# Gates r and z of a GRU as seven block products instead of eight, in a graph-network kernel on one core

## The chip, the core and the metric

The kernel runs on one core of a Trainium2 chip. The metric is the device time of one execution in microseconds (us). A core has five engines that run side by side, each in its own order: TensorE (PE in the profile: matmuls; PEld: its weight loads), VectorE (DVE), ScalarE (ACT), GpSimd (POOL) and SyncE (SP, which here only starts transfers). Matmuls write to PSUM, in banks of 128 partitions x 512 float32; all else lies in SBUF.

## The reference, cut to what matters

64 graphs with 256 nodes and 256 features, float32 throughout. Layer 0 multiplies each graph by its normalised adjacency matrix and a weight, adds the input and normalises (layernorm). Layer 1 makes three things of the result x: a convolution over the nodes with 17 taps (x_conv), messages weighted by a distance (x_nmp), and a GRU cell, which the change is about:

```
x_in = concatenate([x_conv, x_nmp])          # 256 nodes x 512
gi = x_in @ w_ih.T + b_ih                    # 256 x 768: parts r, z, n
gh = x @ w_hh.T + b_hh                       # 256 x 768
r = sigmoid(gi_r + gh_r)
z = sigmoid(gi_z + gh_z)
n = tanh(gi_n + r * gh_n)
out = layernorm(x + (1 - z) * n + z * x)
```

For r and z the hidden and the input part are only added. So both gates together are one product: inputs (256 nodes x 768: x, x_nmp, x_conv) times weights (768 x 512).

## The kernel before, in words

The 64 graphs go in four quarters of Q = 16. `layer0` (L314) and `layer1` (L379) do everything of a graph up to the messages, and write three things to DRAM: x1 (`x1_d`), the gates' inputs x and x_nmp transposed (`xn_d`), and, in SBUF, the Fourier transform, in blocks of nodes, of the convolution's first step (`V`, L436). When a quarter is through, the convolution is done for all its graphs at once: `products` (L504) multiplies each of the 24 frequencies by its weights, streamed from DRAM (`load_u`, L476, on SP's queue); `real_transform` and `complex_begin` start the inverse transform, and `complex_end` (L669) does its rest on VectorE, in 18 pieces, with 16 outputs that go to DRAM (`output`, L655, `xc_d`). Then come the quarter's gates, `gru` (L730), one graph after another: 4 pieces per graph.

`gru` before: for each chunk c of 128 nodes, six matmuls of 128 x 128 weights by 128 x 512 give r and z together in one PSUM bank (L748), and six of half that width give the two parts of n in another (L759). VectorE adds the bias (L763), ScalarE takes tanh (L764; a sigmoid by tanh of half the argument), GpSimd makes z + 3 and multiplies x1 by it (L766, L767), VectorE joins the parts of n (L769 to L773), ScalarE takes its tanh (L776), and VectorE and ScalarE finish with the layernorm (L787 to L789). The convolution reaches the gates by `load_conv` (SP), `residual` (a DMA that adds x1, issued by GpSimd, L715) and `transposed` (four transposes, L726, and two relus on ScalarE, L728, into `xcT`).

What orders the work: each stage is a generator that yields between pieces, and `merge`, `take` and `both` weave them by hand. `AHEAD` graphs (8 before) of the next quarter run layer 0 and 1 during the current quarter's convolution, with their transform in a second buffer `V2`, which is copied into V (L925) when the inverse has left it. The other graphs of the next quarter then run beside the first 4 gates (`early`), and the other 12 gates (`late`) run beside the next quarter's products and inverse. The last quarter has no next one: its gates run alone, at the end. The framework places the waits, gives out buffers, and draws up each engine's order from priorities in the order of the code, so work that is ready can be pulled ahead of its place: the first L748 matmuls run at 413.5 us, while the first inverse outputs (L664) are at 427.3.

PSUM is split into four banks for graphs (`bank`) and four for products and gates (`accbank`).

Of the kernel before, what the change touches and what calls it, by code (L numbers as in the profile page):

```python
# [9 lines left out]
F32 = mybir.dt.float32  # L10
# [4 lines left out]
P = 128  # L15
# [11 lines left out]
def kernel(  # L27
# [47 lines left out]
    loads = ctx.enter_context(tc.tile_pool(name="loads", bufs=3))  # L75
# [42 lines left out]
    unused = const.tile([P, N], F32)  # L118
# [5 lines left out]
    scols = []  # L124
    for i in range(2):
        t = const.tile([P, NCH, P], F32, name=f"scols{i}")
        nc.gpsimd.memset(t, 0.0)
        for c in (NSE, 32 + NSE):
            nc.gpsimd.memset(t[:, :, c : c + 1], 1.0)
        scols.append(t)  # L130

    wih = const.tile([P, 2 * DCH, 3 * D], F32)
    whh = const.tile([P, DCH, 3 * D], F32)
    brz_t = const.tile([P, 2 * D], F32)
# [179 lines left out]
    def layer0(g):  # L314

        a_t, x_t = ain.pop(g), xin.pop(g)


        deg = small.tile([P, NCH], F32, name="deg")
        if g < 2:  # L320
            nc.vector.tensor_reduce(deg, a_t, AX.X, ALU.add)
        else:
            for c in range(NCH):
                nc.scalar.activation(unused, a_t[:, c, :], AF.Copy, accum_out=deg[:, c : c + 1])
# [8 lines left out]
        adjT = work.tile([P, NCH, 3, P], F32, name="adjT", bufs=3)  # L333
        ADJT[g] = adjT
# [44 lines left out]
    def layer1(g, V, place):  # L379
# [23 lines left out]
        cols = scols[g % 2].rearrange("p c (q r) -> p c q r", r=32)  # L403
# [39 lines left out]
        for c in range(NCH):  # L443
            nc.tensor.transpose(p[:, c * P : (c + 1) * P], scols[g % 2][:, c, :], ident)
# [132 lines left out]
    def turned(re, im, angle):  # L577


        t = freq.tile([P, 2, D], F32, name="turn", bufs=4)  # L580
        x, y = M[:, re, :], M[:, im, :]
        real_part(t[:, int(re > im), :], x, y, angle)
        return imaginary_part(t[:, int(re < im), :], x, y, angle), t
# [4 lines left out]
    def real_transform():  # L588
# [17 lines left out]
        for i, x, y in ((1, 9, 13), (2, 10, 14), (3, 15, 11)):  # L606
            angle = math.pi * ORDER[i] / 8
            t = freq.tile([P, 2, D], F32, name="turn", bufs=4)
# [46 lines left out]
    def output(q, n, re, im):  # L655
# [4 lines left out]
        t = freq.tile([P, 2, D], F32, name="turn", bufs=4)  # L660
# [39 lines left out]
    GATE, CONV, XCT = {}, {}, {}  # L700
# [5 lines left out]
    def load_gate(g):  # L706
        x1 = gate.tile([P, NCH, D], F32, name="x1_g")
        nc.sync.dma_start(x1, x1_d[g // Q][g % Q].rearrange("(c p) d -> p c d", p=P))
        xn = gate.tile([P, 2 * DCH, N], F32, name="xn_g")
        nc.sync.dma_start(xn, xn_d[g])  # L710
        GATE[g] = x1, xn
# [7 lines left out]
    def transposed(g):  # L719

        xc = CONV.pop(g)
        XCT[g] = gate.tile([P, DCH, N], F32, name="xcT")
# [4 lines left out]
        for k in range(DCH):  # L727
            nc.scalar.activation(XCT[g][:, k], p[:, k], AF.Relu, bias=bn2_bias[:, k : k + 1])  # L728

    def gru(g):  # L730

        following = g % Q + 1 < Q
        (x1, xn), xcT = GATE.pop(g), XCT.pop(g)
        trz = gate.tile([P, NCH, 2 * D], F32, name="trz", bufs=1)
        nn = gate.tile([P, NCH, D], F32, name="nn", bufs=1)
        if following:
            load_gate(g + 1)
        for c in range(NCH):
            cs = slice(c * P, (c + 1) * P)

            hid = [(xn[:, k, cs], whh[:, k, :]) for k in range(DCH)]
            inp = [(xn[:, DCH + k, cs], wih[:, DCH + k, :]) for k in range(DCH)]
            inp += [(xcT[:, k, cs], wih[:, k, :]) for k in range(DCH)]

            q = accbank("p_rz")
            terms = hid + inp
            for j, (lhsT, w) in enumerate(terms):
                nc.tensor.matmul(q, lhsT, w[:, : 2 * D], start=j == 0, stop=j == len(terms) - 1)  # L748
            if following and c == 1:
                transposed(g + 1)  # L750
            yield
            if following and c == 0:
                residual(g + 1)
# [3 lines left out]
            for o, terms in ((1, hid), (0, inp)):  # L757
                for j, (lhsT, w) in enumerate(terms):
                    nc.tensor.matmul(  # L759
                        p[:, o * D : (o + 1) * D], lhsT, w[:, 2 * D :], start=j == 0, stop=j == len(terms) - 1  # L760
                    )

            nc.vector.tensor_add(trz[:, c, :], q, brz_t)  # L763
            nc.scalar.activation(trz[:, c, :], trz[:, c, :], AF.Tanh, scale=0.5)  # L764
            z3 = gate.tile([P, D], F32, name="z3", bufs=1)
            nc.gpsimd.tensor_scalar(z3, trz[:, c, D:], 3.0, None, op0=ALU.add)  # L766
            nc.gpsimd.tensor_tensor(x1[:, c, :], x1[:, c, :], z3, op=ALU.mult)  # L767
# [3 lines left out]
                gn[:, 1, :], trz[:, c, :D], 1.0, gn[:, 1, :], op0=ALU.add, op1=ALU.mult  # L771
# [14 lines left out]
            y, t, n = x1[:, part], trz[:, part, D:], nn[:, part]  # L786
# [51 lines left out]
    with tc.tile_pool(name="setup", bufs=1) as setup:  # L838
# [10 lines left out]
        def gate_weights():  # L849
            nc.sync.dma_start(whh, w_hhT.rearrange("(k p) o -> p k o", p=P))  # L850
            nc.sync.dma_start(wih, w_ihT.rearrange("(k p) o -> p k o", p=P))
# [3 lines left out]
        others[4] = chain(others[4], gate_weights())  # L855
# [5 lines left out]
        nc.vector.tensor_add(brz_t, bih_t[:, : 2 * D], bhh_t[:, : 2 * D])  # L861
# [7 lines left out]
    AHEAD = Q // 2  # L869
# [3 lines left out]
    def gates(q, part):  # L873

        for i in part:
            if i == 0:
# [7 lines left out]
                yield  # L884
            yield from gru(q * Q + i)
# [5 lines left out]
    for q in range(NQ):  # L891
# [3 lines left out]
        if more:  # L895
            if q:
                others = [both(take(late, 2), take(end, 2)) for _ in range(AHEAD)]
# [18 lines left out]
        elif more:  # L916
            run(merge(merge(take(late, 18), take(begin, 6), 3), take(end, 6), 4))
# [68 lines left out]
```

## Time and profile before

| | us |
|---|---|
| median of three runs | 2233.99 (2231.01 to 2239.59) |
| the profiled execution | 2229.6 |
| its span, first to last instruction | 2227.7 |
| busy: TensorE / VectorE / ScalarE / GpSimd | 2140 / 1347 / 840 / 612 |
| first transform's products and inverse | 310 to 495 |
| late gates, products and inverse, second quarter | 650 to 856 |
| the same, third quarter | 1182 to 1386 |
| the same, last quarter, its late gates to the end | 1708 to 1965 |
| the last 16 gates alone | 1965 to 2228 |

In the profile a row of a group reads: line, engine, operation, output <- input by the program's names, shapes, how often; then the busy time in all and the mean of one in ns. In the busy times by stage a row reads: start and end of the stretch, its length, then for each engine its busy time and (x) its instructions; then the clock that TensorE was granted, the share of the DMA engines and GB/s. In the chain of waits, followed back from the last instruction, a row is the start, the duration, the engine, the line and the number of instructions. A float32 matmul shows as two records, so counts of PE rows are twice those of the code.

### The profile page before, as it was taken

The page shows a single profiled execution, that of the slowest core. Times are in us where ns is not written, and L with a number is a line of the kernel's source. Part 1 is how long each engine was busy: PE and PEld are TensorE (multiplying, and loading weights), DVE is VectorE, ACT ScalarE, POOL GpSimd, SP SyncE. Part 2 cuts the span into 40 slices and gives each one's busy share as a digit, 9 for nine tenths or more (in the row PEclk, how much of TensorE's full clock was granted, in tenths as well). Part 3 has the DMA queues.
Part 4 walks back from the last instruction along what each step waited for, and adds up shares of the span by engine and source line. Part 5 has one row for each costly group of instructions (what it writes and reads, how often), then busy time and mean ns, then how long its engine had stood idle before and what let it go on. Part 6 is the DMA issues. An engine that isn't in the chain of part 4 may idle for free. (4 is left out here: it accounts for less than half of the span.)

```text
span 2227.7 us, 26520 instructions
## 1 busy us (share of the span) xinstructions
PE 2140.2 (96%) x8701; PEld 1533.4 (69%) x8701; DVE 1347.2 (60%) x3487; ACT 839.9 (38%) x1850; POOL 611.9 (27%) x656
## 2 busy tenths in 40 slices
PE   5999989999999999999999999999999999999998
PEld 4777768777767766777667766777776765556555
DVE  6555558895447796545446779545444779644444
ACT  3565633456431124446441122555532112222222
POOL 2344320113211133222221133222221114433332
PEclk9999999999999999999999999999999999999999
DMA  4655667444346644333236655333324655433331
GB/s 121 199 173 158 182 219 235 156 144 125 105 128 194 187 136 136 113 95 111 79 102 181 196 165 146 100 109 109 100 76 128 198 157 141 124 100 99 100 99 52
DMA packets 249732, 305.03 MB, mean 137 GB/s; under 512 B 18458, under 2 KB 227626, under 8 KB 249595
## 3 DMA queue, kind: packets, MB, share of 16 engines
q1 hardware_dynamic: 181500, 199.85, 29.2%
q10 hardware_dynamic: 45280, 68.04, 8.4%
q0 software_dynamic: 22816, 35.45, 8.3%
q8 instruction: 69, 1.13, 0.2%
q14 instruction: 67, 0.55, 0.1%
HBM read 200.71 MB, written 102.57 MB: 136 GB/s over the span
## 5 line engine op out<-in xcount | busy, mean ns | idle before, releaser
L766 POOL TENSOR_SCALAR z<-trz 128x256 f32<-128x256 f32 x128 | 125.0, 977 | 649.9 <-ACT trz L764 649.9
L748 PE MATMUL p_rz<-wih,xcT 128*128 128x512 f32 x512 | 241.3, 593 | 2.2 <-ACT xcT L728 2.2
L748 PE MATMUL p_rz<-wih,xn_g 128*128 128x512 f32 x512 | 243.2, 594 | 0.0
L748 PE MATMUL p_rz<-whh,xn_g 128*128 128x512 f32 x512 | 243.0, 594 | 0.0
L293 POOL TENSOR_TENSOR ln_rs<-ln_rs,neg_half 128x2 f32<-128x2 f32 x129 | 99.0, 767 | 428.9 <-DVE ln_rs L292 371.7
L763 DVE TENSOR_TENSOR trz<-p_rz,brz_t 128x512 f32<-128x512 f32 x128 | 87.7, 686 | 164.5 <-PE p_rz L748 164.4
L776 ACT ACTIVATE nn<-gn 128x256 f32<-128x256 f32 x128 | 53.3, 417 | 351.6 <-DVE gn L773 351.1
L748 PEld LDWEIGHTS p_rz<-wih,xcT 128*128 128x128 f32 x512 | 96.9, 190 | 124.0 <-issue 120.2
L748 PEld LDWEIGHTS p_rz<-wih,xn_g 128*128 128x128 f32 x512 | 96.2, 190 | 118.3 <-issue 118.2
L486 PE MATMUL p_k<-u,VM 128*128 128x256 f32 x736 | 175.2, 380 | 0.8 <-DMA u<-ud 0.7
L769 DVE TENSOR_TENSOR gn<-p_n,bn_t 128x512 f32<-128x512 f32 x128 | 88.1, 688 | 143.3 <-PE p_n L759 143.2
L486 PEld LDWEIGHTS p_k<-u,VM 128*128 128x128 f32 x736 | 138.3, 190 | 24.9 <-issue 4.6
L358 PE MATMUL p_hT<-adjT,x 128*128 128x256 f32 x512 | 126.9, 393 | 19.4 <-DVE adjT L341 11.9
L748 PEld LDWEIGHTS p_rz<-whh,xn_g 128*128 128x128 f32 x512 | 94.6, 190 | 64.8 <-issue 59.6
L303 ACT ACTIVATE x_g<-x_g,ln_mr,ln_rs 128x256 f32<-128x256 f32 x128 | 70.0, 593 | 181.4 <-DVE ln_mr L301 181.4
L764 ACT ACTIVATE trz<-trz 128x512 f32<-128x512 f32 x128 | 80.5, 629 | 152.8 <-DVE trz L763 108.3
L396 PE MATMUL p_conv<-wc,xn 128*128 128x259 f32 x512 | 126.9, 390 | 7.5 <-ACT xn L388 7.5
L759 PE MATMUL p_n<-whh,xn_g 128*128 128x256 f32 x512 | 133.2, 383 | 0.0
L759 PE MATMUL p_n<-wih,xn_g 128*128 128x256 f32 x512 | 131.7, 379 | 0.0
L759 PE MATMUL p_n<-wih,xcT 128*128 128x256 f32 x512 | 131.4, 379 | 0.0
L431 PE MATMUL p_dft<-fwd,h 128*128 128x240 f32 x512 | 117.9, 374 | 13.7 <-ACT h L400 13.3
L462 PE MATMUL p_nmp<-aT,msg 128*128 128x256 f32 x512 | 123.6, 385 | 5.9 <-DVE aT L457 5.9
(149 smaller groups left out, 4123.8 us busy)
## 6 DMA issues: line engine op xcount, KB each, us to landing
u<-ud SPq DMA_DIRECT2D x284, 256.0 KB
xn_d<-xn ACTq DMA_DIRECT2D x64, 512.0 KB
xn_g<-xn_d SPq DMA_DIRECT2D x64, 512.0 KB
adj_t<-in_adj_dram SPq DMA_DIRECT2D x64, 256.0 KB
x_t<-in_x_dram SPq DMA_DIRECT2D x64, 256.0 KB
x_d<-x ACTq DMA_DIRECT2D x64, 256.0 KB
x_g<-x_d SPq DMA_DIRECT2D x64, 256.0 KB
xc_d<-VM SPq DMA_DIRECT2D x64, 256.0 KB
```

The source lines that it names most:

```text
L293: nc.gpsimd.tensor_tensor(rs[:, : len(chunks)], rs[:, : len(chunks)], neg_half[:, : len(chunks)], op=ALU.pow)
L358: nc.tensor.matmul(p[:, k, :], x1[:, mc, k * P : (k + 1) * P], adjT[:, mc, 1 - mc : 3 - mc, :].rearrange("p n q -> p (n q)"), start=mc == ...
L396: nc.tensor.matmul(p, x1T[:, k, c * P : (c + 1) * P], wc1[:, k, :], start=k == 0, stop=k == DCH - 1)
L431: nc.tensor.matmul(p[:, t0 * FL : t1 * FL], h[:, c, k * P : (k + 1) * P], fwd[:, first : first + t1 - t0, :].rearrange("p t f -> p (t f)") ...
L462: nc.tensor.matmul(p[:, k, :], msg[:, mc, k * P : (k + 1) * P], aT[:, mc].rearrange("p n q -> p (n q)"), start=mc == 0, stop=mc == NCH - 1,)
L486: nc.tensor.matmul(p[:, j * D : (j + 1) * D], v[:, k, :], u[:, k, :], start=k == 0, stop=k == DCH - 1)
L748: nc.tensor.matmul(q, lhsT, w[:, : 2 * D], start=j == 0, stop=j == len(terms) - 1)
L759: nc.tensor.matmul(p[:, o * D : (o + 1) * D], lhsT, w[:, 2 * D :], start=j == 0, stop=j == len(terms) - 1)
L763: nc.vector.tensor_add(trz[:, c, :], q, brz_t)
L764: nc.scalar.activation(trz[:, c, :], trz[:, c, :], AF.Tanh, scale=0.5)
L766: nc.gpsimd.tensor_scalar(z3, trz[:, c, D:], 3.0, None, op0=ALU.add)
L769: nc.vector.tensor_add(gn, p.rearrange("p (i d) -> p i d", i=2), bn_t)
```

## The change

The weights of r and z (768 x 512) and the inputs (two chunks of 128 nodes x 768) are each cut into 2 x 2 blocks: A11, A12, A21, A22 are a node chunk by half of the inputs (three k-tiles of 128), the B blocks half of the inputs by r or z. Strassen's method in Winograd's form gives the four blocks of the product by seven block products instead of eight. Four of those need sums of A blocks, which GpSimd makes for each graph (`input_sums`), and four need sums of B blocks, made once, on VectorE in the setup. The block products end in four PSUM banks (one of them half used), and VectorE puts them together. The bias goes along as two rows, that of r and the difference of z and r. The gates n are computed as before, after both chunks' r and z.

Around it: z + 3 and its product with x1 become one VectorE instruction; the degree pass of layer 0 writes into adjT and not into a tile of its own; loads of x and adj have two buffers instead of three, `turn` three instead of four, `scols` one instead of two; `AHEAD` is 6 instead of 8; and the weaving takes 14 + 20 late pieces where it took 16 + 18, with 5 inverse pieces beside the 20 (one after each five) where there were 6 beside the 18 (one after each four). A graph's gates still have four pieces.

```diff
-    loads = ctx.enter_context(tc.tile_pool(name="loads", bufs=3))
+    loads = ctx.enter_context(tc.tile_pool(name="loads", bufs=2))
...
-                nc.scalar.activation(unused, a_t[:, c, :], AF.Copy, accum_out=deg[:, c : c + 1])
+                nc.scalar.activation(adjT[:, c, 0:2, :].rearrange("p n q -> p (n q)"), a_t[:, c, :], AF.Copy, accum_out=deg[:, c : c + 1])
...
+    def halves(inputs):
+
+        return [inputs[:, i * HALF : (i + 1) * HALF, c * P : (c + 1) * P] for c in range(2) for i in range(2)]
+
+    def input_sums(g):
+        A11, A12, A21, A22 = halves(GATE[g][1])
+        S = SUMS[g] = gate.tile([P, 4, HALF, P], F32, name="sums", bufs=1)
+        nc.gpsimd.tensor_tensor(S[:, 2], A11, A21, op=ALU.subtract)
+        nc.gpsimd.tensor_tensor(S[:, 0], A21, A22, op=ALU.add)
+        nc.gpsimd.tensor_tensor(S[:, 1], S[:, 0], A11, op=ALU.subtract)
+        nc.gpsimd.tensor_tensor(S[:, 3], A12, S[:, 1], op=ALU.subtract)
...
-            q = accbank("p_rz")
-            terms = hid + inp
-            for j, (lhsT, w) in enumerate(terms):
-                nc.tensor.matmul(q, lhsT, w[:, : 2 * D], start=j == 0, stop=j == len(terms) - 1)
-            if following and c == 1:
-                transposed(g + 1)
-            yield
...
+        def block(p, j, a, b):
+            for k in range(HALF):
+                nc.tensor.matmul(
+                    p[:, j * D : (j + 1) * D], a[:, k], wrz[:, b, k], start=k == 0, stop=k == HALF - 1
+                )
+
+        p15, p26 = accbank("p_rz"), accbank("p_rz")
+        block(p15, 0, A11, B11)
+        block(p26, 0, A12, B21)
+        block(p15, 1, S[:, 0], T1)
+        block(p26, 1, S[:, 1], T2)
+        yield
+        if following:
+            residual(g + 1)
+        first = gate.tile([P, 2, D], F32, name="first", tag="gn")
+        nc.vector.tensor_add(first, half(p15), brz_t)
+        nc.vector.tensor_add(trz[:, 0:2], first[:, 0:1].to_broadcast([P, 2, D]), half(p26))
+        p7, p34 = accbank("p_rz"), accbank("p_rz")
+        block(p7, 0, S[:, 2], T3)
+        block(p34, 0, S[:, 3], B22)
+        block(p34, 1, A22, T4)
+        nc.vector.tensor_add(trz[:, 3], trz[:, 1], p7[:, :D])
+        nc.vector.tensor_add(trz[:, 1:3], trz[:, 1:4:2], half(p34))
+
+        nc.scalar.activation(trz[:, 0:4:2], trz[:, 0:4:2], AF.Tanh, scale=0.5)
+        nc.vector.tensor_add(trz[:, 1:4:2], trz[:, 1:4:2], first[:, 1:2].to_broadcast([P, 2, D]))
+        nc.scalar.activation(trz[:, 1:4:2], trz[:, 1:4:2], AF.Tanh, scale=0.5)
+        if following:
+            transposed(g + 1)
+        yield
         for c in range(NCH):
...
+            if c == 0 and following:
+                input_sums(g + 1)
...
-            nc.vector.tensor_add(trz[:, c, :], q, brz_t)
-            nc.scalar.activation(trz[:, c, :], trz[:, c, :], AF.Tanh, scale=0.5)
-            z3 = gate.tile([P, D], F32, name="z3", bufs=1)
-            nc.gpsimd.tensor_scalar(z3, trz[:, c, D:], 3.0, None, op0=ALU.add)
-            nc.gpsimd.tensor_tensor(x1[:, c, :], x1[:, c, :], z3, op=ALU.mult)
...
+            nc.vector.scalar_tensor_tensor(y, t, 3.0, y, op0=ALU.add, op1=ALU.mult)
...
+            for to, a, b in ((T3, B22, T1), (T1, T1, B11), (T2, B22, T1), (T4, B21, T2)):
+                nc.vector.tensor_sub(wrz[:, to], wrz[:, a], wrz[:, b])
...
-    AHEAD = Q // 2
+    AHEAD = 6
...
-                others = [both(take(late, 2), take(end, 2)) for _ in range(AHEAD)]
+                others = [both(take(late, 3 if i % 3 == 0 else 2), take(end, 2)) for i in range(AHEAD)]
...
-            run(merge(merge(take(late, 18), take(begin, 6), 3), take(end, 6), 4))
+            run(merge(merge(take(late, 20), take(begin, 6), 3), take(end, 5), 5))
```

## The prediction

> **What bounds the kernel now.** I read the page's busy table first, then the end of the chain of waits, then the busy time of each engine by stage, then single groups of instructions.
>
> ```profile
> span 2227.7 us, 26520 instructions
> PE 2140.2 (96%) x8701; PEld 1533.4 (69%) x8701; DVE 1347.2 (60%) x3487; ACT 839.9 (38%) x1850; POOL 611.9 (27%) x656
> ```
>
> A busy PE need not be a PE at its rate, so I look at its pace in the chain that ended last (start, duration, what):
>
> ```profile
> 2012.95 5.15 PE p_rz L748 x12
> 2018.10 2.59 PE p_n L759 x12
> 2020.68 5.15 PE p_rz L748 x12
> ```
>
> Rows follow each other without a gap: 12 records of 128x512 take 5.15 us, 429 ns each; 12 of 128x256 take 2.59 us, 216 ns each. (The group rows count 512 records for whh,xn_g where the code issues 256: a float32 matmul is two records.) So a pass half as wide costs half, plus about 1 ns. Adding up the starts of neighbouring matmuls over the whole trace, all that exceeds this pace is 132 us, of which 24 lie in the first 40 us: TensorE works at its rate nearly everywhere, and matmuls taken away are time taken away, if nothing else becomes late.
>
> What could be late is seen by stage (start:end, us, then busy us of PE, PEld, DVE, ACT, POOL with counts; clock, DMA share, GB/s):
>
> ```profile
> 410.00:495.00 85.00, 78.38 (x359) 59.00 (x358) 81.08 (x229) 42.76 (x99) 15.40 (x14) 1.00 0.39 130
> 650.00:767.00 117.00, 116.33 (x462) 86.39 (x461) 81.37 (x160) 21.88 (x43) 22.06 (x24) 1.00 0.68 202
> 767.00:856.00 89.00, 88.44 (x305) 54.58 (x303) 84.35 (x211) 22.67 (x50) 30.81 (x28) 1.00 0.51 143
> 1825.00:1914.00 89.00, 86.81 (x283) 51.50 (x282) 83.42 (x199) 18.07 (x37) 38.65 (x27) 1.00 0.45 127
> 1914.00:1965.00 51.00, 51.00 (x173) 31.23 (x172) 26.29 (x61) 14.39 (x29) 19.48 (x23) 1.00 0.44 115
> 1965.00:2228.00 263.00, 254.46 (x830) 151.65 (x828) 117.87 (x271) 64.28 (x131) 83.12 (x97) 0.99 0.34 90
> ```
>
> In four stretches VectorE is busy 94 to 95%: the ends of the inverse transforms (410-495, 767-856, 1297-1386, 1825-1914). In the last three TensorE still loses nothing to speak of, because the inverse's 61 us of VectorE work are only filler there and late gates keep TensorE fed. In the first there are no late gates and TensorE is busy 78 of 85 us: VectorE is the bound.
>
> **The change, part by part.**
>
> Matmuls. Per graph, r and z take 24 records of 429 ns = 10.30 us. Seven blocks of three k-tiles, 256 wide, are 21 matmuls = 42 records of 216 ns = 9.06 us. The row for that pace is p_n's, with the same weight loads (190 ns, inside the 216). Saved: 1.24 us a graph, times 64 = 79 us. p_n and the transposes stay.
>
> VectorE. Removed per graph: two L763 at 686 ns = 1.37 us. Added: three adds of 128x512 with a PSUM operand (686 each), one of 128x256 (397, the row of L529), one of 128x512 in SBUF (689, L788) and the x1 product, moved from GpSimd (702, L787) = 3.85 us. Net +2.5 us a graph, 158 us in all; VectorE's share rises from 60 to about 69%. Beside TensorE's 14.7 us of a gate (9.06+5.18+0.44) VectorE then has about 10 us: hidden wherever gates run alone.
>
> ScalarE: the two tanh stay 128x512 each. Its degree pass writes adjT instead of a scratch tile: that buffer's last readers are a graph behind, nothing.
>
> GpSimd. Removed: two L766 (977) and two L767 (878) = 3.7 us. Added: four sums of 128x384. POOL rows lie at 878 ns for 128x256 and 1340 for 128x512 (L351), so about 1.1 us each, 4.4 us: net +0.7. But L766 and L767 fed only x1, and the sums feed TensorE. Where gates run alone: the transposes of the next graph end, ScalarE's two relus take 0.9 us, then two POOL sums 2.2 us until S0, a third until S1. TensorE meanwhile has both p_n (5.18 us) and two blocks that need no sum (2.59): S0 is wanted 7.8 us after the transposes and is there after 3.2; S1 is wanted at 9.1 and there at 4.3. Slack 4.6 to 4.8 us. Cost zero; hidden by p_n. Behind the waiting sums on GpSimd stand the layernorm's power (L293) and the residual's DMA issue (L715, 1.26 us): the first delays only an output, the second has nearly a whole gate of lead (L715 at 2013.7, its transposes at 2025.7).
>
> The Trainium skill speaks against these sums: GPSIMD Engine Reference, Engine selection, puts elementwise work with two inputs on VectorE, GpSimd being about twice as slow, and its Specifications say that the two share their SBUF interfaces when VectorE reads two SBUF inputs. The trace agrees with both: 878 ns against 420 for VectorE's 128x256, and L767 (POOL busy us and count) is stretched from 0.77 us where gates run alone to 1.72 beside the inverse:
>
> ```profile
> 1825.00:1914.00 89.00, 15.48 (x9) 1.00 0.45 127
> 1965.00:2228.00 263.00, 25.36 (x33) 0.99 0.34 90
> ```
>
> By the free rows the four sums are 4.4 us, by the stretched ones 9.8; S1 then comes at 0.9+7.4 = 8.3 us, 0.8 us before it is wanted. By the rule they would cost VectorE about 2.2 us a graph more where it is the scarce engine. I take the stretched row there: just in time, but with no slack for a late relu, and those exist: at 1896 the relu came 8 us after its transposes, behind ScalarE work that waited for VectorE, and TensorE lost 2.2 us.
>
> The last transform (1825-1965). 8.5 late gates and 18 inverse pieces. Before, sums of VectorE durations are 126 us, TensorE 138. After: 126 + 8.5 x 2.5 = 147 of VectorE durations, against 8.5 x 14.7 = 125 us of TensorE. Durations overlap: in the saturated stretches their sum is 1.10 to 1.16 of the elapsed time, so 147 need 127 to 134 us. VectorE becomes the bound there by 2 to 9 us. And the last inverse output, done at 1913 under 52 us of late gates, now comes near the last late gate; the next gate needs it written, loaded, added and transposed, some 10 us, half of them filled by matmuls that need no convolution. I take 12 us of loss (5 to 22). The change in the piece counts only spreads the inverse thinner; the sum stays.
>
> The two middle transforms. Same saturation beside 5 late gates, but the inverse can run on under the following graphs, at 50% VectorE, 150 us before V is copied. Only the late relu/sums hurt: 3 us each, from 0 to 10.
>
> The first transform, AHEAD 8 to 6. Two graphs (13.5 us TensorE, some 7 us VectorE each) leave a stretch that VectorE bounds. It shortens by 14/1.13 = 13 us, TensorE's work by 27; most of the difference is filled by work pulled forward (the trace shows such pulling: L748 ran first at 413.5 us, while its xcT came at 518.9). Cost 8 us, from 3 to 14.
>
> Loads with two buffers: in the steady order the slot is free when the load is issued; only the third graph of a quarter waits for the first one's end. SP's queue carries the u loads behind it, six deep: 2 us, from 0 to 6. Setup: eleven weight DMAs for two, of the same bytes, and four subtractions of 128x768 (0.95 us each), in a stretch where VectorE is busy 53%: zero, cover TensorE's 243 of 257 us; 4 us without it. Buffers of turn, scols: zero, VectorE takes them in order. PSUM: a gate now holds two of the four accumulator banks per step, freed by adds just behind; inside the ranges above. Tail: the last p_n and what follows are unchanged, zero.
>
> Sum: 79 - (12 + 3 + 3 + 8 + 2) = 51 us. The profiled execution took 2229.6 us (span 2227.7); less 51 it is 2179. The median is 4.4 us above that execution; so 2183.
>
> **Rivals.**
> 1. All of it arrives: the inverse stays filler and the work pulled forward fills the first transform. For it: before, 95% VectorE cost TensorE under 3 us per stretch. Losses 3 us: 2234 - 79 + 3 = 2158. Chance 0.24.
> 2. The forecast, 2183. Chance 0.50.
> 3. GpSimd's sums are late beside the inverse: 18.5 gates lie there (5+5+8.5); with 2 us each, 37 us more, less the 6 I counted: 2214. For it: the stretched L767, the late relu. Against: TensorE's order has other work between gates in the middle transforms. Chance 0.18.
> 4. Slower: the same place, with VectorE and GpSimd each blocking the other, so that relu and sums come a full chain late: 5 us per gate for those 18.5 gates is 93 us, giving 2234 - 79 + 93 = 2248. It turns the sign from 4.3 us per gate (79/18.5). One L767 of 3.9 us (at 1891.6, its longest) shows that it can be; that their mean there is 1.7 speaks against. Chance 0.08.
>
> **How the numbers follow.** A measurement can tell about 0.5% from no change: 2223 to 2245. Cases 1 and 2 lie below, case 3 with two thirds, case 4 above. Faster 0.87, same 0.06, slower 0.07. The range takes in case 1 with a little room and reaches over case 3: 2155 to 2220.
>
> **What would show it.** p_rz at 216 ns a record and 42 records a graph; gates alone every 14.7 us instead of 15.9. VectorE near 1505 us. TensorE waiting for POOL sums only beside the inverse. A gap before the first gate of the last quarter, and TensorE busy less than 78 of 85 us in the first inverse. I am wrong if the 256-wide passes take over 216 ns, if TensorE waits for sums where gates run alone, or if the last stretch keeps its 140 us less 10.

## The result and the profile after

The changed kernel takes 2215.65 us, median of four runs (2214.26 to 2217.32), beside 2232.5 us for the kernel before (2227.95 to 2239.59): a ratio of 0.992, 95% interval 0.989 to 0.995. That is 17 us less where 51 were forecast, and it lies inside the range, near its upper end.

The head of the page and the busy table of the kernel after:

```profile
span 2214.4 us, 29080 instructions
PE 2077.4 (94%) x9853; PEld 1753.5 (79%) x9853; DVE 1564.9 (71%) x3749; ACT 835.9 (38%) x1850; POOL 670.2 (30%) x653
```

VectorE is the surprise: 218 us more than before, where 158 were planned. TensorE did what the forecast said. I gave every matmul record of each trace its pace (216 ns for 256 columns, 429 for 512, and so on) and added up: 2081.8 us before, 2002.7 after, so 79.1 us saved, and the saving forecast was 79. What the distances between neighbouring records exceed that pace by is TensorE's loss: 129.6 us before, 193.8 after. Of the 79 us, 64 were lost again.

The busy times by stage of the kernel after, in the columns of the prediction's view (start:end, us, PE, PEld, DVE, ACT, POOL, clock, DMA share, GB/s):

```profile
411.00:497.00 86.00, 65.83 (x310) 52.60 (x308) 77.27 (x210) 34.33 (x79) 11.56 (x10) 0.93 0.44 141
782.00:912.00 130.00, 115.66 (x526) 97.50 (x525) 126.14 (x285) 35.12 (x77) 48.11 (x42) 0.96 0.45 131
1301.00:1432.00 131.00, 115.34 (x532) 96.89 (x532) 126.31 (x287) 35.70 (x77) 48.51 (x42) 0.97 0.46 131
1819.00:1953.00 134.00, 118.68 (x547) 99.92 (x546) 129.88 (x268) 29.05 (x59) 47.97 (x43) 1.00 0.38 107
1953.00:2214.00 261.00, 249.50 (x1181) 217.38 (x1179) 183.99 (x362) 66.88 (x140) 106.69 (x102) 0.99 0.39 102
```

In rows two to four, the inverse transforms beside late gates, VectorE is busy 96 to 97% and TensorE only 88 to 89%; before, the same stages had TensorE at 97 to 99%. In the last row the gates run alone: VectorE has room, and from 2000 us on TensorE loses nothing. The loss by stage, in us, from the same distances in bins of 50 us (the bounds, us from the span's start, take in each kernel's stage, which lies a little earlier or later in each; "elsewhere" is the rest):

| kernel | setup, 0-350 | first inverse, 350-550 | second, 800-950 | third, 1300-1450 | last, 1800-2000 | elsewhere | sum |
|---|---|---|---|---|---|---|---|
| before | 55.7 | 20.9 | 9.2 | 8.9 | 2.4 | 32.5 | 129.6 |
| after | 66.7 | 35.5 | 24.1 | 22.6 | 24.0 | 20.9 | 193.8 |

What does TensorE wait for? The longest of its waits by cause (line, what it waited for, us in all, times, longest), after:

```profile
PE p_dft L431 <- ACT h L400: 27.2, 20, 9.6
PE p_n L793 <- DVE first L769: 15.7, 13, 2.4
...
PE p_conv L396 <- ACT xn L388: 12.2, 9, 3.9
PE p_rz L756 <- DVE gn L798: 9.8, 9, 1.6
PE p_rz L756 <- POOL sums L738: 9.4, 8, 2.5
```

Waits for GpSimd's sums (L738) are 9.4 us, one in seven of the 64. The rows for L769 and L798 are waits for VectorE to empty a PSUM bank. So the profile says "VectorE late", and not yet why.

### The profile page after: what moved, and what is told of

Read it like the earlier page. It is cut to its first block, busy times and chain, and to the rows that moved or that the text cites. A ratio compares the mean times of both kernels' runs of the same rounds, so it can differ in the third digit from the quotient of the medians.

```text
span 2214.4 us, 29080 instructions
## 1 busy us (share of the span) xinstructions
PE 2077.4 (94%) x9853; PEld 1753.5 (79%) x9853; DVE 1564.9 (71%) x3749; ACT 835.9 (38%) x1850; POOL 670.2 (30%) x653
## 4 chain that ended last, share of the span: by engine, by line
PE 50%; DVE 13%; issue 6%; POOL 5%; ACT 4%; DMA 0%; ACTq 0%; POOLq 0%; SPq 0%; DVEq 0%
PE p_rz L756 18%; PE p_n L793 9%; PE p_k L486 8%; PE p_nmp L462 3%; PE p_out L368 2%; PE p_dft L431 2%; PE p_conv L396 2%; PE p_hT L358 2%; PE p_msg L417 1%; POOL sums L738 1%; POOL ln_rs L293 1%; PE p_dist L455 1%; POOL sums L740 1%; POOL sums L739 1%; DVE gn L798 1%
## 5 line engine op out<-in xcount | busy, mean ns | idle before, releaser
L756 PE MATMUL p_rz<-wrz,sums 128*128 128x256 f32 x1536 | 356.0, 383 | 19.5 <-DVE gn L798 9.8
L793 PE MATMUL p_n<-wn,inputs 128*128 128x256 f32 x1536 | 351.3, 381 | 16.3 <-DVE first L769 15.7
L756 PEld LDWEIGHTS p_rz<-wrz,sums 128*128 128x128 f32 x1536 | 288.6, 191 | 70.9 <-issue 15.8
L793 PEld LDWEIGHTS p_n<-wn,inputs 128*128 128x128 f32 x1536 | 285.7, 190 | 62.2 <-DVE first L769 18.9
L756 PE MATMUL p_rz<-wrz,inputs 128*128 128x256 f32 x1152 | 272.8, 380 | 2.1 <-ACT inputs L728 1.5
L756 PEld LDWEIGHTS p_rz<-wrz,inputs 128*128 128x128 f32 x1152 | 216.8, 190 | 33.7 <-ACT inputs L728 3.6
L737 POOL TENSOR_TENSOR sums<-inputs 128x384 f32<-128x384 f32 x64 | 70.0, 1093 | 241.6 <-issue 172.0
L431 PEld LDWEIGHTS p_dft<-fwd,h 128*128 128x128 f32 x512 | 95.9, 192 | 44.0 <-ACT h L400 36.4
L368 PE MATMUL p_out<-w,hT 128*128 128x256 f32 x512 | 124.4, 386 | 1.3 <-ACT hT L363 1.1
L396 PEld LDWEIGHTS p_conv<-wc,xn 128*128 128x128 f32 x512 | 98.0, 194 | 31.5 <-ACT xn L388 16.4
L417 PE MATMUL p_msg<-wmsg,xn 128*128 128x256 f32 x512 | 122.0, 381 | 0.0
```

The source lines that it names most:

```text
L368: nc.tensor.matmul(p[:, c, :], hT[:, k, c * P : (c + 1) * P], w0[:, k, :], start=k == 0, stop=k == DCH - 1)
L396: nc.tensor.matmul(p, x1T[:, k, c * P : (c + 1) * P], wc1[:, k, :], start=k == 0, stop=k == DCH - 1)
L417: nc.tensor.matmul(p[:, c, :], x1T[:, k, c * P : (c + 1) * P], wmsg[:, k, :], start=k == 0, stop=k == DCH - 1)
L431: nc.tensor.matmul(p[:, t0 * FL : t1 * FL], h[:, c, k * P : (k + 1) * P], fwd[:, first : first + t1 - t0, :].rearrange("p t f -> p (t f)") ...
L756: nc.tensor.matmul(p[:, j * D : (j + 1) * D], a[:, k], wrz[:, b, k], start=k == 0, stop=k == HALF - 1)
L793: nc.tensor.matmul(p[:, o * D : (o + 1) * D], lhsT, w, start=j == 0, stop=j == len(part) - 1)
```

## The experiments

At first I held three theories for the stages beside the inverse, and the expectations call them by letters. V: the adds that put the blocks together fill VectorE. G: GpSimd's sums are the cost. A: AHEAD 6 instead of 8 costs the first inverse. D is the degree pass that now writes adjT, for the setup. Later the question became in which way the sums cost. All runs, with the ratio to the kernel before on the same chip:

| kernel | what is different from the kernel after | us | ratio, 95% | VectorE busy | GpSimd busy |
|---|---|---|---|---|---|
| no_sums | no sums; blocks read inputs | 2149.63 | 0.964 (0.963 to 0.965) | 1468.7 | 374.0 |
| light | most of the recombination left out | 2200.89 | 0.987 (0.985 to 0.988) | 1452.6 | 667.1 |
| before_ahead6 | kernel before, AHEAD and weaving of after | 2244.62 | 1.0065 (1.005 to 1.008) | 1355.1 | 616.3 |
| deg_own | degree pass has its own tile again; one weight buffer fewer | 2223.40 | 0.996 (0.995 to 0.998) | 1572.2 | 685.8 |
| sums_unread | sums made, read by nobody | 2211.94 | 0.993 (0.991 to 0.995) | 1565.6 | 684.9 |
| sums_one_input | GpSimd copies instead of sums | 2173.73 | 0.975 (0.974 to 0.977) | 1498.0 | 697.4 |
| sums_dve | sums on VectorE | 2195.24 | 0.985 (0.984 to 0.987) | 1583.4 | 373.3 |
| sums_split | two sums on VectorE, two on GpSimd | 2207.11 | 0.990 (0.989 to 0.992) | 1596.9 | 515.5 |
| late16 | sums_dve, 16 gates kept for the last transform, inverse pieces spread thinner | 2187.64 | 0.981 (0.979 to 0.983) | 1583.9 | 372.7 |
| late14 | the same with 14 | 2190.34 | 0.982 (0.980 to 0.984) | 1581.6 | 372.5 |
| sums_thirds | each sum in three instructions; one execution | 2215.05 | | 1538.5 | 796.8 |

And TensorE's loss by stage for those that the argument uses, as above:

| kernel | setup | first inverse | second | third | last | elsewhere | sum |
|---|---|---|---|---|---|---|---|
| no_sums | 64.3 | 29.8 | 7.4 | 7.1 | 2.9 | 15.0 | 126.5 |
| light | 65.5 | 34.0 | 23.1 | 21.5 | 17.7 | 16.0 | 177.8 |
| sums_unread | 67.5 | 31.2 | 24.7 | 23.8 | 21.5 | 20.6 | 189.3 |
| sums_one_input | 68.4 | 35.1 | 11.4 | 12.5 | 10.5 | 17.7 | 155.6 |
| sums_dve | 68.1 | 32.4 | 15.0 | 15.2 | 28.7 | 14.2 | 173.6 |
| late16 | 67.5 | 32.6 | 15.0 | 15.8 | 2.0 | 34.2 | 167.1 |
| before_ahead6 | 59.0 | 31.2 | 5.7 | 5.4 | 4.1 | 44.0 | 149.4 |

**Sums or recombination (no_sums, light).**

```diff
-        S = SUMS[g] = gate.tile([P, 4, HALF, P], F32, name="sums", bufs=1)
-        nc.gpsimd.tensor_tensor(S[:, 2], A11, A21, op=ALU.subtract)
...
+        SUMS[g] = A21, A22, A11, A12
```

> The changed kernel without GpSimd's four sums: the block products take input blocks in their place, so r and z are not the reference's; the number of matmuls and VectorE's adds are unchanged. Theory V (VectorE is what TensorE waits for beside the inverse): the waits for sums (9 us) go, and what GpSimd takes from VectorE by sharing (some 60 us of VectorE durations, a third of it beside the inverse); 8 to 15 us faster than the changed kernel, 2201 to 2208. Theory G (the sums are the cause, by their lateness and by their load): the stretches beside the inverse lose next to nothing, 35 us or more faster, 2181 or less.

```diff
-        nc.vector.tensor_add(first, half(p15), brz_t)
-        nc.vector.tensor_add(trz[:, 0:2], first[:, 0:1].to_broadcast([P, 2, D]), half(p26))
+        nc.vector.tensor_add(trz[:, 0:2], half(p15), brz_t)
+        nc.vector.tensor_add(trz[:, 2:4], half(p26), brz_t)
...
-        nc.vector.tensor_add(trz[:, 3], trz[:, 1], p7[:, :D])
-        nc.vector.tensor_add(trz[:, 1:3], trz[:, 1:4:2], half(p34))
...
-        nc.vector.tensor_add(trz[:, 1:4:2], trz[:, 1:4:2], first[:, 1:2].to_broadcast([P, 2, D]))
```

> The changed kernel with VectorE's recombination left out: two adds of 128x512 per graph as before, banks three and four never read, so r and z are not the reference's; matmuls and GpSimd's sums stay. VectorE has 1.8 us less per gate, 114 us in all. Theory V: the three stretches with late gates lose little more than before (their 45 us of loss fall to 10 or so), and the whole is 25 to 40 us faster than the changed kernel, 2176 to 2191; the first inverse and the setup keep their losses. Theory G: those stretches still wait for sums, and the gain is under 12 us.

Without the sums the kernel is 66 us faster than after, 81 faster than before. The busy table of no_sums:

```profile
PE 2057.2 (96%) x9853; PEld 1750.2 (82%) x9853; DVE 1468.7 (68%) x3749; ACT 837.2 (39%) x1850; POOL 374.0 (17%) x397
```

VectorE runs the same 3749 instructions as after, on the same shapes, and is busy 96 us less. Its second inverse, to be held against 782-912 of the kernel after:

```profile
772.00:886.00 114.00, 110.78 (x529) 96.36 (x528) 109.02 (x287) 35.76 (x77) 17.52 (x18) 0.99 0.52 150
```

287 VectorE instructions here and 285 there: 109 us of work against 126. The 17 us more of VectorE are the 16 us by which that stage is longer. And TensorE's waits in no_sums have lost the rows for L769, L798 (L765 and L794 here) and the sums; the list goes on below, but no PSUM bank of the gates stands in it with more than 1 us:

```profile
PE p_dft L431 <- ACT h L400: 22.7, 17, 8.8
...
PE p_conv L396 <- ACT xn L388: 8.1, 5, 3.2
...
PE p_n L789 <- DVE trz L766: 1.0, 1, 1.0
```

light keeps the sums and takes 112 us of busy time from VectorE. It gains only 15 us (V had 25 to 40, G under 12), and the second and third stage lose about as much as after (23.1 and 21.5). Theory V falls: the recombination is in no_sums too, whole, and there these stages lose no more than before the change. Theory G stands. VectorE's total does not decide: light's 1452.6 us are fewer than the 1468.7 of no_sums, and light is 51 us slower. What does decide, the next experiment shows.

**Late, or in the way (sums_unread).** G could mean that TensorE waits for the sums, or that making them slows VectorE.

```diff
-        S = SUMS[g] = gate.tile([P, 4, HALF, P], F32, name="sums", bufs=1)
+        S = gate.tile([P, 4, HALF, P], F32, name="sums", bufs=1)
...
+        SUMS[g] = A21, A22, A11, A12
```

> The changed kernel with GpSimd's four sums made as they are, but read by nobody: the block products take input blocks in their place (r and z are not the reference's). Without the sums it took 2150 us, with them 2216; this run splits those 66 us. Theory C (contention: GpSimd's two-input sums hold up VectorE's instructions with two SBUF inputs, and VectorE is what TensorE waits for beside the inverse): VectorE's busy time stays near 1565 us and the whole at 2195 to 2212. Theory L (lateness: TensorE, whose order is fixed, stands behind a block whose sum is not there): 2150 to 2165, VectorE's durations being hidden.

2211.94 us: of the 66 us between after and no_sums, 62 are there although no matmul reads a sum, nor waits for one; that is theory C, at the upper end of its range. The cost is not lateness. It is what the sums do to VectorE:

```profile
PE 2077.1 (94%) x9853; PEld 1755.7 (79%) x9853; DVE 1565.6 (71%) x3749; ACT 836.2 (38%) x1850; POOL 684.9 (31%) x653
```

1565.6 us of VectorE, as after (1564.9). To see which instructions grow, three groups of VectorE in the kernel after (busy us, mean ns, idle before):

```profile
L798 DVE TENSOR_TENSOR gn<-p_n,bn_t 128x512 f32<-128x512 f32 x128 | 87.4, 683 | 15.9 <-PE p_n L793 15.3
...
L816 DVE SCALAR_TENSOR_TENSOR x_g<-trz,x_g 128x512 f32<-128x512 f32 x63 | 57.0, 905 | 24.3 <-ACT trz L780 24.0
...
L779 DVE TENSOR_TENSOR trz<-trz,first 128x512 f32<-128x512 f32 x64 | 52.5, 820 | 1.4
```

and the same three in no_sums:

```profile
L794 DVE TENSOR_TENSOR gn<-p_n,bn_t 128x512 f32<-128x512 f32 x128 | 88.0, 688 | 39.5 <-PE p_n L789 38.7
...
L775 DVE TENSOR_TENSOR trz<-trz,first 128x512 f32<-128x512 f32 x64 | 44.1, 689 | 1.4
...
L812 DVE SCALAR_TENSOR_TENSOR x_g<-trz,x_g 128x512 f32<-128x512 f32 x63 | 43.1, 684 | 24.0 <-ACT trz L776 23.9
```

Without sums all three take 684 to 689 ns. With them the two whose inputs both lie in SBUF take 820 and 905, and the one that reads p_n from PSUM still 683. The timeline of the kernel after shows single cases (start, us, engine, line):

```profile
1844.88 1.42 POOL L738 TENSOR_TENSOR sums<-inputs 128x384 f32<-128x384 f32 x1 [1.63 <-ACT inputs L728]
...
1845.35 0.68 DVE L798 TENSOR_TENSOR gn<-p_n,bn_t 128x512 f32<-128x512 f32 x1
...
1846.37 1.32 POOL L739 TENSOR_TENSOR sums<-sums,inputs 128x384 f32<-128x384 f32 x1
1846.77 1.21 DVE L799 SCALAR_TENSOR_TENSOR gn<-trz,gn 128x256 f32<-128x256 f32 x1
...
1847.78 1.06 POOL L740 TENSOR_TENSOR sums<-inputs,sums 128x384 f32<-128x384 f32 x1
1847.90 1.22 DVE L564 SCALAR_TENSOR_TENSOR turn<-VM 128x256 f32<-128x256 f32 x1
1849.04 0.41 DVE L802 SCALAR_TENSOR_TENSOR gn<-gn 128x256 f32<-128x256 f32 x1
```

L798, from PSUM, runs under a sum at its usual 0.68 us. L799 and L564 begin under a sum and take 1.21 and 1.22 us, until just after the sum's end; L802, a 128x256 too, begins when none runs and takes 0.41. Over the whole trace, of VectorE's instructions that begin while a sum runs: 128x256 with two inputs in SBUF (gn, turn, VM) 810 ns on average, at most 1219, against 431 for the others of that kind; 128x512 (L816, L779) 1023, at most 1489, where no_sums has 684 to 689; 128x512 with an input in PSUM 680 against 681.

The ends say more than the averages. Of the 96 of 128x256, 70 take over 450 ns, and all 70 end 276 to 286 ns after the end of the sum that they met, whenever they began; of 79 of 128x512 (the same outputs, L816 and L779), the 64 that take over 720 ns end 544 to 553 ns after it. The other 26 of 128x256 keep their usual length; the sums that they met are the long ones, 2.3 us on average (a sum counts once for each instruction that met it), where all sums take 1.18.

Where do VectorE's 96 us lie? Take from each instruction the median of its group in no_sums; what is left is its stretch (groups that no_sums lacks are left out). Of it, 92.5 us lie in instructions that begin while a sum runs. By stage, in the bounds of the loss table, with TensorE's loss beside it (us; second, third and last transform; for sums_one_input, which follows below, copies stand for sums):

| kernel | stretch under sums, whole trace | stretch by stage | TensorE's loss by stage |
|---|---|---|---|
| after | 92.5 | 14.9, 16.6, 23.0 | 24.1, 22.6, 24.0 |
| sums_unread | 93.8 | 14.8, 15.9, 24.6 | 24.7, 23.8, 21.5 |
| light | 85.9 | 14.4, 16.4, 22.7 | 23.1, 21.5, 17.7 |
| sums_one_input | 29.9 | 5.7, 4.6, 6.9 | 11.4, 12.5, 10.5 |
| no_sums | none | 0.3, 0.8, -0.7 | 7.4, 7.1, 2.9 |

In the second and third stage TensorE loses more than in no_sums by what VectorE is stretched more, to 3 us; in the last stage the two differ by up to 9. This fits light's small gain: it has less VectorE work, but the stretch stays.

**The kind of GpSimd's work (sums_one_input).** This kernel copies one input where the other adds two: as many GpSimd instructions on the same shapes.

```diff
-        nc.gpsimd.tensor_tensor(S[:, 2], A11, A21, op=ALU.subtract)
...
+        for n, a in ((2, A11), (0, A21), (1, A22), (3, A12)):
+            nc.gpsimd.tensor_scalar(S[:, n], a, 1.0, None, op0=ALU.mult)
```

> The changed kernel with GpSimd making four scaled copies of input blocks (one input each, same sizes, read by the block products) in place of the four sums, so r and z are not the reference's. Is it two inputs that hold up VectorE? If so (Theory C with the port shared only by two-input work), VectorE's rows shrink to what they were without sums, 1470 to 1490 us, and the whole takes 2155 to 2175. If any GpSimd work of that length does it, VectorE stays near 1565 us and the whole at 2200 to 2220. Theory L: as late as before, 2200 or more, whatever VectorE's rows do.

2173.73 us. GpSimd is busy longer than with the sums, as the group of its copies shows (1280 ns each, the four sums 1093 to 1223),

```profile
L738 POOL TENSOR_SCALAR sums<-inputs 128x384 f32<-128x384 f32 x256 | 321.8, 1280 | 264.7 <-issue 173.5 <-ACT inputs L728 38.6 <-PE p_rz L754 30.3
```

where the kernel after has

```profile
L738 POOL TENSOR_TENSOR sums<-inputs 128x384 f32<-128x384 f32 x64 | 78.2, 1222 | 122.5 <-ACT inputs L728 122.5
```

and yet 38 of the 62 us are back. VectorE's 128x256 that begin under a copy take 461 ns against 429, its 128x512 (the same adds as L816 and L779) 740, and it is busy 1498 us in all (1470 to 1490 expected). So most of the cost comes from the two inputs of GpSimd's instruction, beside two of VectorE's in SBUF; the kind of instruction changed with the number of inputs, and the two were not separated. A copy does not leave VectorE alone: 24 of 145 of 128x256 take over 450 ns, and the stretch under copies is 30 us, near the 29 by which VectorE is busier than in no_sums. So a third of the stretch stays. Of the 24 us of time that remain to no_sums, how much comes from it was not measured.

**The length of GpSimd's instruction (sums_thirds).** Each sum in three of 128x128.

```diff
-        nc.gpsimd.tensor_tensor(S[:, 2], A11, A21, op=ALU.subtract)
...
+            for k in range(HALF):
+                nc.gpsimd.tensor_tensor(S[:, to, k], a[:, k], b[:, k], op=op)
```

> The changed kernel with each of GpSimd's four sums cut into three of 128x128; all is computed. In the changed kernel VectorE's 128x256 instructions with two SBUF inputs that start under a sum take 0.73 to 0.89 us in the mean and up to 1.5, instead of 0.42. If VectorE waits for the end of GpSimd's instruction, the longest falls to about 1.1 us (0.42 and one short sum of 0.65), and as GpSimd's work grows to some 7.8 us a gate, the whole stays at 2205 to 2225. If they merely share the port word by word, the length of an instruction does not matter: the longest stays at 1.5 us.

VectorE's longest case under a sum falls from 1219 and 1489 ns (128x256; 128x512 in L816 and L779) to 764 and 995, the means from 810 and 1023 to 594 and 841. The distance from the end of the sum to the end of the held instruction stays: 281 and 547 ns at the median, where it was 281 and 546. So VectorE's instruction waits for the end of the sum that it met, and a shorter sum lets it go earlier. But more of them meet one (281 where there were 155, of the groups named), GpSimd's time rises by 127 us, and the time of the kernel stays: 2215.05 in one execution.

**Where the sums should be (sums_dve, sums_split).** All four, or two, on VectorE:

```diff
-        nc.gpsimd.tensor_tensor(S[:, 2], A11, A21, op=ALU.subtract)
+        nc.vector.tensor_tensor(S[:, 2], A11, A21, op=ALU.subtract)
...
```

> The changed kernel with the four sums of each graph on VectorE in place of GpSimd; all is computed. At 0.55 us for 128x384 they are 2.2 us a gate, 141 us in all. Theory C: VectorE loses 141 us to its own work and is spared the 96 us that it lost to sharing, so it is busier by some 45 us, but the sums are never late: within 12 us of the changed kernel, 2204 to 2228. Theory L: the sums come quickly, right after the relu, and the gain of most of the 66 us returns: 2160 to 2185.

> The changed kernel with the two sums that TensorE wants first (S0, S1) on VectorE and the other two on GpSimd; all is computed. Theory C: half the sharing (48 us less on VectorE) against 70 us of its own sums: about the same as the changed kernel, 2206 to 2226. Theory L: the two early sums no longer wait for GpSimd: 2165 to 2190.

On VectorE a sum takes 549 to 569 ns, 142.6 us for all 256. VectorE's busy time is 1583.4 us, 18.5 more than with the sums on GpSimd: handing 302 us of work to GpSimd relieved VectorE of 18.5 us. And the kernel with the busier VectorE is 20 us faster than after; the second and third stage lose 15 us each, not 24 and 23, while the last loses 28.7. With two sums moved the time lies between, at 2207.11, though VectorE is then the busiest of all (1596.9). The time of sums_dve lies between the two theories' (2204 to 2228 and 2160 to 2185), so neither foresaw it. Of the 28.7 us in the last stage, 18.2 are two waits ahead of the last quarter's first gate, 9.5 for its first sum and 8.7 for the transfer that brings its convolution. Why the busier VectorE loses less in the middle stages is not shown. It is not the amount of work: the sums take 15.4 and 13.7 us of VectorE there, about as much as the stretch that they replace (14.9 and 16.6). That the order of its work is drawn up with the sums in it, whereas a wait for GpSimd is in nobody's plan, is an argument only.

**The last transform (late16, late14).** In sums_dve the last stage has too few gates for its inverse. These two keep all 16, or 14, gates of the third quarter for it, where the other had 12.

```diff
-            early = gates(q, range(EARLY))
+            count = EARLY if q + 2 < NQ else 0
+            early = gates(q, range(count))
...
-            run(merge(late, end, 2))
+            run(merge(late, end, 3))
```

> The kernel with the sums on VectorE (2195 us), and the third quarter's 16 gates all kept for the last transform (before: 12 there, 4 beside the graphs), with one inverse piece after each three gate pieces; all is computed. In the last stretch that kernel lost 27 us of TensorE's pace. Theory V2 (what is left is VectorE's work beside the last inverse: a gate has 14.7 us of TensorE and 12.3 us of VectorE durations, 10.9 elapsed, so 3.8 us to spare, and 54 us of inverse need 14 gates): the last stretch loses 5 to 10 us and the whole takes 2175 to 2185. Rival (the graphs that lose their gates lose as much): 2190 to 2205.

> The same with 14 of the third quarter's gates kept for the last transform. Theory V2: between the two, 2178 to 2190. Rival: 2190 to 2200.

2187.64 and 2190.34 us: late16 between the two theories, late14 just inside the rival's. The last stage of late16 has TensorE busy throughout:

```profile
1800.00:1935.00 135.00, 133.79 (x636) 117.05 (x635) 125.12 (x303) 35.55 (x72) 17.42 (x18) 1.00 0.46 129
```

It loses 2.0 us instead of 28.7, but the last quarter's graphs, which had four gates beside them, lose 20 us more ("elsewhere", 34.2 against 14.2). The net gain is 7.6 us, where theory V2 had 10 to 20. late16 is the fastest version here that computes the whole: 42 us below the kernel before, 28 below after.

**The first inverse (before_ahead6).** The kernel before, with AHEAD and weaving of after alone:

```diff
-    AHEAD = Q // 2
+    AHEAD = 6
...
-            run(merge(merge(take(late, 18), take(begin, 6), 3), take(end, 6), 4))
+            run(merge(merge(take(late, 20), take(begin, 6), 3), take(end, 5), 5))
```

> The kernel before with AHEAD 6 and the weaving of the changed kernel, and nothing else of it. It asks what the six graphs alone cost. Theory A (the first inverse is bound by VectorE and lacks two graphs of TensorE work): 8 to 16 us slower than before, all of it between 410 and 520 us, with one gap in front of p_dft; the stretches with late gates stay as they are. Rival (the longer second half of each quarter gives it back): within 4 us of before.

14 us slower than before, as theory A had it. The first inverse loses 31.2 us where it lost 20.9; that this is all of the loss, as the theory said, is not so. In this trace, of the slowest execution (2250.53 us), 11.5 us more are lost elsewhere, 3.3 in the setup and 1.7 in the last stage, and 7.0 less in the second and third. So theory A holds for the first inverse alone. In the kernel after the gap lies at 479.9 us, where a Fourier transform's matmuls wait 9.6 us for h (the longest of the first row of waits above). From 484 to 496 us VectorE is busy without a pause, as the theory has it: the six graphs are used up before the inverse's VectorE work. What follows shows at once:

```profile
484.00:508.00 24.00, 13.23 (x32) 9.14 (x33) 16.29 (x47) 9.64 (x18) 4.46 (x4) 0.50 0.36 102
```

TensorE's granted clock is 0.50 over these 24 us, and neighbouring 128x256 records start 427 ns apart in place of 216. Matmuls at half pace are some 4 us of the 14.6 that this stage loses more than before.

**The setup (deg_own).** The degree pass gets its tile back; to make room the stream of convolution weights has five buffers, not six.

```diff
+    unused = const.tile([P, N], F32)
...
-                nc.scalar.activation(adjT[:, c, 0:2, :].rearrange("p n q -> p (n q)"), a_t[:, c, :], AF.Copy, accum_out=deg[:, c : c + 1])
+                nc.scalar.activation(unused, a_t[:, c, :], AF.Copy, accum_out=deg[:, c : c + 1])
...
-    ustream = ctx.enter_context(tc.tile_pool(name="ustream", bufs=6))
+    ustream = ctx.enter_context(tc.tile_pool(name="ustream", bufs=5))
```

> The changed kernel with the degree pass writing into a tile of its own again, as before (for its 1 KB the weight stream has five buffers, not six). It asks where 11 us of the setup went: products of the first transform start at 321 us after the change, at 310 before. Theory D (the degree pass now waits for an adjT buffer that the messages of an earlier graph still read): the products start at 310 to 312 and the whole takes 2205 to 2210 us, from 2216. Rival (the order of the setup is disturbed by the two load buffers, the one scols tile or the weight sums): they start at 319 or later and the whole stays within 3 us of the changed kernel.

The kernel after shows what the degree pass waits for, over the whole trace (us in all, times, longest):

```profile
ACT adjT L326 <- DVE aT L457: 37.1, 43, 2.7
```

L457 is the product on VectorE that reads adjT: only then is the buffer free. The first product starts at 310.2 us before, 321.3 after, 315.6 here and 314.4 in before_ahead6: about 6 of the 11 us are the degree pass, about 4 the other AHEAD, by single traces. Theory D had 310 to 312 and a faster kernel (2205 to 2210), so it is shown for about half of the setup's delay only. As a whole deg_own is 8 us slower than after. The missing sixth buffer is in the traces: TensorE waits for convolution weights, in deg_own and in the kernel after:

```profile
PE p_k L487 <- DMA u<-ud: 13.0, 17, 2.2
PE p_k L486 <- DMA u<-ud: 0.8, 1, 0.8
```

These 12 us more outweigh the 6 gained. A run with six buffers and the tile, which would separate them, was not made.

## Why the prediction was off

The gain was right to the microsecond (79.1 against 79), and so were its reasons: 216 ns a record, a gate alone every 14.7 us, no loss where gates run alone. VectorE's recombination was right too: it costs next to nothing, even in the last stage, where the forecast gave it up to 9 us (no_sums loses 2.9 there, before the change 2.4). What failed is the losses, 64 us against 28. That the time still lies in the range is luck: the range reached that far for late sums, and the sums cost their time in another way.


- **The step that failed is the price of GpSimd's sums.** The prediction quoted that the two engines share their SBUF interfaces, and it named what that does to VectorE: "about 2.2 us a graph more where it is the scarce engine". Then it took the stretched L767 for the length of the sums alone, asked whether a sum comes in time ("just in time, but with no slack"), and put the 2.2 us into no stage's sum: the last transform is reckoned with 2.5 us of VectorE a gate, the recombination, and the middle ones with late sums only. The runs show that term: about 96 us of VectorE time, 62 us of the kernel's. Charged as it stood, for 18.5 gates, it is 41 us, and the forecast by this estimate 2224, 8 us from the measured time and not 33. It could be read before the change: in that trace VectorE's 128x256 with two inputs in SBUF (gn, turn, VM) that begin under an L767 take 562 ns on average (52 of them, at most 950), against 430 for the others, and L767's 1.72 us was a sign that each waits for the other. VectorE "near 1505" became 1565; no_sums, without any such work, has 1469.
- Second and third transform: 3 us each forecast; 14.9 and 13.7 more than before measured, nothing of it in no_sums. "The inverse can run on under the following graphs" did not help: TensorE's order has the gates' matmuls in it, and they wait for their PSUM banks.
- Last transform: 12 forecast (5 to 22), 21.6 measured. The size was inside the bounds, the cause was another one: not too much VectorE work, but VectorE work made longer. The gap before the last quarter's first gate, of which a part of the 12 was made, is not there: none of TensorE's waits in that stage is over 1.6 us.
- First inverse: 8 forecast (3 to 14), 14.6 measured, 10.3 of it from AHEAD alone by before_ahead6. The mechanism was right, the size just above the upper end; the clock behind the gap, some 4 us, was not in the sum. (14/1.13 is 12, not 13; that changes nothing.)
- Setup: nothing forecast, 11.0 measured. "That buffer's last readers are a graph behind, nothing" was the step for about half of it: those readers were not done. In the setup a graph is taken every 17.2 us where it was 16.5, with the degree pass waiting for L457. The other part is AHEAD, as above.
- Loads with two buffers, 2 us: not seen by itself. Elsewhere TensorE loses 11.6 us less than before, which no step of mine had and no run explains.

Sum of the changes by stage: 11.0 + 14.6 + 14.9 + 13.7 + 21.6 - 11.6 = 64 us, so 79 - 64 = 15 us, with the medians 17 apart.

Rival 3 named 2214 us, and the time is there, but its mechanism is not: sums that nobody waits for cost nearly as much. Rival 4 had the two engines blocking each other, but took it to act through late sums, and its size was too large. With sums, the last three transforms lose 53 us more than without (70.7 against 17.4); by its 18.5 gates that is 2.9 us a gate, short of the 4.3 from which the sign would turn.

The rule weighed in the prediction has a sharper form in the Trainium skill, SBUF — State Buffer, section "SBUF: two separate sides": the shared pair of ports is locked for a whole instruction by whichever engine starts first, and a VectorE instruction with two inputs in SBUF takes part if GpSimd's reads SBUF. The traces agree for the sums: a held instruction of VectorE ends at a fixed distance after the sum, and one with an input in PSUM is not held. By that rule every sum can hold up VectorE by up to its length, 302 us in all as the upper bound (an estimate from the sums' durations); the trace makes 96 of it. Where they differ, the measurement decides: GpSimd's copies read SBUF as well, and yet 121 of 145 of VectorE's 128x256 that began under one took no more than 450 ns, and the 24 that were held ended 386 to 389 ns before the copy's end, not after it.

## What to carry to other kernels

Work given to GpSimd is relief for VectorE only as far as VectorE's time falls: with two inputs in SBUF on both sides, 302 us of GpSimd's work cost VectorE 96 us of waiting, where doing it itself cost 115 (1583.4 against 1468.7). Before forecasting such a move, split the durations of VectorE's groups by whether GpSimd runs a two-input instruction beside them, and where VectorE is near 95% busy, charge the difference. And a stage that is full needs the price of both directions of a shared resource, not only of the one whose lateness would be seen.

## What the hardware showed unexpectedly

- A VectorE instruction of 128x256 with two inputs in SBUF, beginning under a two-input GpSimd sum of 1.1 to 1.2 us, took 810 ns on average instead of 431, and if it was held it ended 276 to 286 ns after the sum; with an input in PSUM there was no difference (680 and 681 for 128x512). The block goes the other way too: one L738, 1.2 us on average, took 3.88 us at 845.4 us, while VectorE ran without a pause and at its usual lengths; it ended 0.94 us after VectorE began its first instruction with an input in PSUM, L798 at 848.34.
- In a gap of 9.6 us TensorE's granted clock fell to 0.50, some 4 us after the gap began, and stayed there for 24 us, though matmuls ran for 13 of them. Around gaps of about 4 us (from 884 and 1403 us) it was 0.50 for 6.8 us. A gap of TensorE costs more than its length.
